# A four-block model on one Trainium2 core: where the attention's weighted values and adapter scores are transposed, and into which banks

## Chip, cores and metric

The kernel runs on one core of a Trainium2 chip. The core has TensorE (PE, matrix products and transposes, with its own queue of weight loads, PEld), VectorE (DVE), ScalarE (ACT), GpSimd (POOL) and the queues that start transfers (SP among them). The metric is the device time of one execution in microseconds (us); lower is better. Products and transposes land in PSUM, which has eight banks of 2 KB for each of the 128 partitions: a bank takes 512 float32 numbers a partition.

## The reference, cut to what matters

The input is 4 sequences of 256 tokens with 512 channels. Four blocks follow each other; the change is in the first, an attention with 32 heads of 16 channels and an adapter: ten learned extra keys and values with a softmax of their own, gated and added.

```
q, k, v = split(layernorm(x) @ w_attn.T); q, k = rope(q), rope(k)
scores  = q @ k.T / sqrt(hd)                    # causal mask, hd = 16
y       = softmax(scores) @ v
ascores = gating * softmax(q @ ak.T / sqrt(C))  # ak, av: 10 adapter keys and values per head
y       = (y + ascores @ av) @ w_proj.T
x = x + y
x = x + ffn(layernorm(x)); x = x + mixer(layernorm(x)); x = x + ffn(layernorm(x))
```

## The kernel before, in words

All of the attention lies in one function. The 4 sequences (batches, b) are done in 8 steps of 4 heads each (u), 32 steps i = 8b + u in one loop. Four heads share the 128 partitions in PE's array, 32 rows a head. For one step there are these stages; line numbers are those of the kernel before.

1. *Scores* (L492): 16 products into four PSUM banks (pool of 4, tile `sc`), one bank a head, of which 384 of 512 columns are used: 256 columns for the second half of the queries (c = 1), 128 for the first (c = 0). DVE reads them in eight reduces (L500), which add the causal mask, write the scores to on-chip memory as `e` and leave the row maximum in `nmx`. ACT then takes eight exponentials (L508).
2. *turn* (L523), one step later: 12 transposes of the exponentials into three banks `ptr`, copied out as `eT` (L524), the first and third by ACT and the second by DVE.
3. *weigh* (L533, L539), two steps later: the exponentials times the values into the bank `py`; a column of ones among the values gives the softmax's sum. DVE copies py out as `ys` (L547, function `taken`).
4. *gathered* (L553), three steps later: two transposes `try` turn ys back to tokens on partitions; DVE takes the reciprocal of the sum, `ry` (L558), and multiplies into the batch's result `y` (L559). `y` has one buffer: the next batch's first write must wait until the batch before is read out.

Beside that runs, in steps of even u (except the very first step) and once at the start, the adapter: *adapter_scores* makes products `pa` (L457), ACT copies them out as `sa` (L462), two transposes `tra` (L466) turn them, and ACT copies the result into the batch's `as` (L467). There are four such pieces a batch. After the fourth, at u = 7, *adapted* (L570 to L577) makes the adapter's softmax on all of `as`: a maximum `anm` on DVE, an addition on POOL, an exponential on ACT, sum `asum`, reciprocal and scaling on DVE, a multiplication on POOL. In the next batch's first step its transposes `pt` (L584) follow, and then its products with the adapter values, `pya`.

*closed* adds the two parts of a batch and turns the result for the output projection (transposes `try2`, named try in the profile, L610, with copies `yT`, L107 and L108). Three quarters of it are done in the step in which the batch's seventh `gathered` is finished (steps 10, 18, 26), the last one a step later (steps 11, 19, 27); its transposes go into the stage "turn", at a step's end.

Other long products (`pq` for queries, keys and values of the next batch, `po`, and parts of the next block) are placed by hand into the stage "long" of a step (12 products of 128x512, L115 to L117); transposes of the queries and keys (`trp`, L444, copied out as `pc` and swapped by DMA) come just after the scores.

The order on PE is written out by hand in the loop. In a step i it is: scores(i), adapter products, trp, long products, weigh(i - 2), turn(i - 1), try of gathered(i - 3), tra, then the stage "turn" (pt, the transposes of the next normalised rows `tr`, the closed batch's try2). The order on DVE, ACT and POOL is made by a scheduler from the dependencies.

Of the eight PSUM banks three are a rotating pool "m": ptr, try, tra, try2, pa, pt, pq, trp and the rest take its banks in turn, and a transpose into a bank waits until the copy out of it three tiles earlier is done. Four are the score banks, one tile each, and one is for py.

Of the kernel before, what the change touches and what calls it, by code (L numbers as in the profile page):

```python
# [20 lines left out]
P = 128  # L21
# [58 lines left out]
def hybrid_kernel(  # L80
# [190 lines left out]

    def attention(later, region):
        with ExitStack() as es:
            inner, banks = ExitStack(), ExitStack()
            pool = lambda name, bufs, **kw: es.enter_context(tc.tile_pool(name=name, bufs=bufs, **kw))
            w1 = pool("a_w", 1)
            p1 = pool("a1", 1)
            p2 = pool("a2", 2)
            p3 = pool("a3", 3)
            ps, ps_s, ps_y = (  # L280
                banks.enter_context(tc.tile_pool(name=name, bufs=bufs, space=PSUM))
                for name, bufs in (("a_m", 3), ("a_s", 4), ("a_y", 1))
            )

            acon = w1.tile([P, NCOL_ATTN - NCOL_KEEP], F32, name="acon")
# [150 lines left out]
            def pieces(b, q, f):  # L436
# [13 lines left out]
                turned_.setdefault((b, q), []).append(o)  # L450
                yield

            def adapter_scores(b, q):
                pa = ps.tile([AW, L], F32, name="pa", tag="m")
                for j in range(4):
                    n = (4 * q + j) * AW
                    nc.tensor.matmul(  # L457
                        pa, akbd[:, n : n + AW], turned_[b, q][0][:, 0, j % 2, :],
                        start=(j == 0), stop=(j == 3),
                    )  # L460
                sa = p2.tile([AW, 4, P], F32, name="sa", tag="paT").rearrange("p s i -> p (s i)")[:, :L]
                nc.scalar.copy(sa, pa)  # L462
                yield
                tr = ps.tile([P, 2, AW], F32, name="tra", tag="m")
                for c in range(2):
                    nc.tensor.transpose(tr[:, c, :], sa[:, c * P : (c + 1) * P], ident[:AW, :AW])  # L466
                nc.scalar.copy(  # L467
                    state[b]["as"][:, :, q * 8 : q * 8 + 8, :].rearrange("p c h a -> p c (h a)"), tr
                )
# [11 lines left out]
            def scores(b, u):  # L481

                qT, kT = turned_[b, u // 2]
                es_ = [p2.tile([P, 4, (c + 1) * P], F32, name=f"e{c}", tag=f"e{c}") for c in range(2)]
                tops = {}
                banks_ = [ps_s.tile([P, 3, P], F32, name="sc", tag="sc") for _ in range(4)]
                for c, at in ((1, slice(0, 2)), (0, slice(2, 3))):
                    n = (c + 1) * P
                    for v in range(2):
                        for r in range(4):  # L490
                            rows = slice(32 * r, 32 * r + 32)
                            nc.tensor.matmul(  # L492
                                banks_[r][:, at, :].rearrange("p k i -> p (k i)"),
                                qT[rows, 0, u % 2, c * P : (c + 1) * P], kT[rows, v, u % 2, :n],
                                start=(v == 0), stop=(v == 1),
                            )
                for c, at in ((1, slice(0, 2)), (0, slice(2, 3))):
                    tops[c] = nm = p3.tile([P, 4], F32, name="nmx", tag="nmx", bufs=4)
                    for r in range(4):
                        nc.vector.tensor_tensor_reduce(  # L500
                            es_[c][:, r, :].rearrange("p (k i) -> p k i", i=P), banks_[r][:, at, :],
                            mask[:, 1 - c :, :], -1.0, 3e38, ALU.add, ALU.min, nm[:, r : r + 1],
                        )

                yield
                for c in (1, 0):
                    for r in range(4):
                        nc.scalar.activation(  # L508
                            es_[c][:, r, :], es_[c][:, r, :], AF.Exp, scale=-1.0, bias=tops[c][:, r : r + 1],
                        )  # L510
                    if c == 0:
                        all_es[8 * b + u] = es_
                    yield
# [34 lines left out]
                return ys  # L548

            def gathered(b, u, ys):  # L550
                tr = ps.tile([P, 2, 4, 32], F32, name="try", tag="m")
                for c in range(2):
                    nc.tensor.transpose(  # L553
                        tr[:, c].rearrange("p h d -> p (h d)"), ys[:, c * P : (c + 1) * P], ident
                    )
                st = state[b]
                ry = p2.tile([P, 2, 4], F32, name="ry")
                nc.vector.reciprocal(ry, tr[:, :, :, HD])  # L558
                nc.vector.tensor_tensor(  # L559
                    st["y"][:, :, 64 * u : 64 * u + 64].rearrange("p c (h d) -> p c h d", h=4),  # L560
                    tr[:, :, :, :HD], ry.unsqueeze(3).to_broadcast([P, 2, 4, HD]), ALU.mult,
                )
# [137 lines left out]
                norm.stats(t, tc.keep_in_program_order)  # L700
            norm.root(2, TT)
            begin(0)
            for f in range(2):
                for _ in pieces(0, 0, f):
                    pass
            part = pieces(0, 1, 0)
            next(part)
            moved(adapter(), -1)
            with tc.manual_schedule(engines={nc.tensor.engine}):
                for i in range(n):  # L710
                    b, u = divmod(i, 8)
                    if u == 0:
                        if i:
                            begin(b)
                        if b + 1 < B:
                            moved(prepared(b + 1), i)
                    scoring = scores(b, u)
                    next(scoring)
                    if i in FEEDS:
                        moved(fed(feed, FEEDS[i]), i - 1)  # L720
                    if i == 2:
                        nc.scalar.activation(a_s, a_s, AF.Exp)
                        nc.gpsimd.tensor_scalar(a_s, a_s, -1.0, None, ALU.mult)
                    if i == 3:
                        weights(wp_s, wproj, "ya", nc.gpsimd, p1)
                    if u % 2 == 0 and i > 0:
                        asides.append(adapter_scores(b, u // 2))
                        next(asides[-1])
                    if part:
                        next(part)  # L730
                    part = None
                    next(scoring)
                    step("long", i)
                    step("values", i)
                    if 2 <= i:
                        py = weigh(*divmod(i - 2, 8), eTs.pop(i - 2))
                    if 1 <= i:
                        eTs[i - 1] = turn(all_es.pop(i - 1))
                    next(scoring)
                    if 2 <= i:  # L740
                        yss[i - 2] = taken(py)
                    if 3 <= i:
                        gathered(*divmod(i - 3, 8), yss.pop(i - 3))
                    while asides:
                        next(asides.pop(0), 0)
                    step("turn", i)
                    if u == 7:
                        moved(adapted(b), i)
                    if 3 <= i:
                        if (i - 3) % 8 == 6:  # L750
                            moved(closed((i - 3) // 8, (0, 1, 2)), i)
                        if (i - 3) % 8 == 7:
                            moved(closed((i - 3) // 8, (3,)), i)

                    b, u = divmod(i + 3, 8)
                    if b < B:
                        part = pieces(b, u // 2, (i + 1) % 2)
                        next(part)
                    if i == 23:
                        inner.close()  # L760
                        feed = Feed("f", *(
                            later.enter_context(
                                tc.tile_pool(name=f"f{v}", bufs=v, side="right", reuse_waits="tile")
                            ) for v in (1, 2)
                        ))
                    if i in range(23, 27):
                        feed.weights(i - 23, nc.gpsimd)
                        feed.norm.stats(i - 23)
                    if i == 26:
                        feed.norm.root(0, 4)  # L770
# [3 lines left out]
                step("long", n)  # L774
                yss[n - 2] = taken(weigh(b, 6, eTs.pop(n - 2)))
                eTs[n - 1] = turn(all_es.pop(n - 1))
                gathered(b, 5, yss.pop(n - 3))
                step("turn", n)
                moved(fed(feed, 3), n - 1)
                step("turn", n)  # L780
                step("long", n + 1)
                step("values", n + 1)
                yss[n - 1] = taken(weigh(b, 7, eTs.pop(n - 1)))
                gathered(b, 6, yss.pop(n - 2))
                moved(closed(b, (0, 1, 2)), n)
                moved(fed(feed, 4), n)
                step("turn", n + 1)
                gathered(b, 7, yss.pop(n - 1))
                moved(closed(b, (3,)), n)
                step("long", n + 2)  # L790
                step("turn", n + 2)
# [1120 lines left out]
```

## Time and profile before

| what | us |
|---|---|
| median of 3 runs | 1805.35 (1804.81 to 1807.16) |
| profiled execution | 1805.61 |
| its span | 1803.8 |
| first scores of the loop to the last step's scores | 31.7 to 280.6 |
| PE busy from 28 to 318 | 262.88 of 290.00 |

The steps have different lengths, since the long products differ. The start of the score products, read from PE's timeline:

| step | 10 | 11 | 12 | 13 | 18 | 19 | 20 | 26 | 27 | 28 |
|---|---|---|---|---|---|---|---|---|---|---|
| first score product at | 117.67 | 126.03 | 132.99 | 140.36 | 181.11 | 189.41 | 196.38 | 243.91 | 250.38 | 255.07 |

ScalarE's row for the copy of the adapter scores is one of the operations that move in order: all 16 of them in the trace.

```profile
L467 ACT COPY as<-tra x16: 281/292/298, 64.7 to 279.9; 128x160 f32<-128x160 f32 x16
L570 DVE TENSOR_REDUCE anm<-as x4: 819/820/821, 93.6 to 280.3; 128x64 f32<-128x640 f32 x4
L571 POOL TENSOR_TENSOR as<-as,anm x4: 1293/1300/1529, 94.5 to 281.2; 128x640 f32<-128x640 f32 x4
L584 PE MATMUL pt<-con,as x32: 272/273/280, 106.5 to 299.5; 128*80 128x128 f32 x32
```

In this view, of all that touches the tile `as`, the three numbers after the count are the shortest, the median and the longest duration in ns, followed by the start of the first and the last of them in us and the operands' shapes. In a timeline the columns are start, duration, engine, line, operation, written tile and read tiles, count; in square brackets stands how long the engine was idle before, and what it waited for.

### The profile page before, as it was taken

To read this page: it belongs to the slowest core of one execution; us is meant where nothing else is said; L and a number is where in the kernel's file an instruction comes from. 1 tells how busy PE (TensorE), PEld (TensorE's weight loads), DVE (VectorE), ACT (ScalarE), POOL (GpSimd) and SP (SyncE) were. 2 spreads that over 40 slices of the span, in tenths; PEclk is the share of its full clock that TensorE was granted. 3 is DMA by queue.
4 is the path that set the end of the run, shared out by engine and by line. 5 is a ranking of instruction groups with operands and counts; after the bars stand their busy time and mean duration, and the time that the engine had idled before them with its cause. 6 is when DMAs were issued, how large, how long until landed. Compare 5 with 4: busy or idle time off the path is not lost.

```text
span 1803.8 us, 33220 instructions
## 1 busy us (share of the span) xinstructions
PE 1745.7 (97%) x12862; PEld 1417.8 (79%) x12862; DVE 1427.7 (79%) x2523; ACT 1268.7 (70%) x2293; POOL 240.9 (13%) x249
## 2 busy tenths in 40 slices
PE   7999988899999999999999999999999999999998
PEld 6777767778877888888888888888888888888877
DVE  5676676889998788787878797878788878887777
ACT  5676684578887668766866686668667867777754
POOL 5332320111110111011110101110111101101100
PEclk8999999999999999999999999999999999999999
DMA  4000100122344234423433252325333433343231
GB/s 157 19 19 19 47 26 26 43 71 99 109 127 137 80 106 154 120 85 99 153 100 100 88 162 90 109 81 176 103 94 112 135 106 94 115 138 115 85 97 56
DMA packets 136941, 173.71 MB, mean 96 GB/s; under 512 B 12752, under 2 KB 78032, under 8 KB 136784
## 3 DMA queue, kind: packets, MB, share of 16 engines
q1 hardware_dynamic: 127712, 138.57, 25.5%
q10 hardware_dynamic: 9072, 33.03, 4.8%
q8 instruction: 101, 1.65, 0.4%
q14 instruction: 56, 0.46, 0.1%
HBM read 131.71 MB, written 35.65 MB: 93 GB/s over the span
## 4 chain that ended last, share of the span: by engine, by line
PE 76%; DVE 11%; ACT 8%; issue 3%; DMA 1%; POOL 1%; SPq 0%; ACTq 0%; DVEq 0%; POOLq 0%
PE pp L115 13%; PE pp L117 12%; PE pp L116 12%; PE pyy L1252 7%; PE pog L115 6%; PE pog L117 6%; PE pog L116 6%; PE trx L1233 3%; DVE acc L980 2%; ACT e L508 1%; ACT em L1213 1%; DVE em L1226 1%; PE pq L115 1%; PE ptr L523 1%; PE pq L117 1%
## 5 line engine op out<-in xcount | busy, mean ns | idle before, releaser
L115 PE MATMUL pp<-mx,w 128*128 128x512 f32 x1144 | 459.3, 401 | 0.0
L117 PE MATMUL pp<-mx,w 128*128 128x512 f32 x1144 | 446.8, 391 | 0.0
L116 PE MATMUL pp<-mx,w 128*128 128x512 f32 x1144 | 446.1, 390 | 0.0
L1285 POOL TENSOR_TENSOR sq<-sq,x 128x1024 f32<-128x1024 f32 x54 | 132.1, 2446 | 1177.7 <-ACT x L1284 1177.7
L117 PEld LDWEIGHTS pp<-mx,w 128*128 128x128 f32 x1144 | 214.7, 188 | 46.2
L115 PEld LDWEIGHTS pp<-mx,w 128*128 128x128 f32 x1144 | 214.8, 188 | 44.7
L980 DVE SCALAR_TENSOR_TENSOR acc<-pp,cw_s,acc 128x1012 f32<-128x1012 f32 (+2 forms) x192 | 244.5, 1274 | 4.3
L116 PEld LDWEIGHTS pp<-mx,w 128*128 128x128 f32 x1144 | 215.1, 188 | 40.5
L1226 DVE TENSOR_TENSOR em<-em,gm 128x1280 f32<-128x1280 f32 x128 | 189.5, 1489 | 72.1 <-ACT em L1221 72.1
L115 PE MATMUL pog<-wo,gh 128*128 128x512 f32 x512 | 201.2, 393 | 2.0 <-DVE x L1381 2.0
L117 PE MATMUL pog<-wo,gh 128*128 128x512 f32 x512 | 200.2, 391 | 0.9 <-DVE gh L1364 0.9
L116 PE MATMUL pog<-wo,gh 128*128 128x512 f32 x512 | 199.8, 390 | 0.0
L1236 DVE TENSOR_TENSOR xd<-trx,dt_t 128x512 f32<-128x512 f32 x128 | 82.4, 685 | 141.5 <-PE trx L1233 141.5
L1152 ACT ACT_TABLE_LOAD x63 | 80.8, 1283 | 139.1 <-DVE acc L980 138.9
L1443 ACT ACTIVATE gt<-pp 128x1024 f32<-128x1024 f32 x64 | 65.6, 1025 | 145.0 <-PE pp L117 145.0
L1252 PEld LDWEIGHTS pyy<-em,xd 64*64 64x64 f32 x4096 | 130.2, 133 | 44.2 <-issue 17.6
L1213 ACT ACTIVATE em<-r,end_t 128x128 f32<-128x128 f32 x512 | 163.1, 389 | 0.8
L1252 PE MATMUL pyy<-em,xd 64*64 64x256 f32 (+3 forms) x4096 | 157.8, 300 | 3.1 <-DVE em L1226 3.0
L115 PEld LDWEIGHTS pog<-wo,gh 128*128 128x128 f32 x512 | 96.3, 188 | 24.8 <-issue 2.8
L508 ACT ACTIVATE e<-e,nmx 128x256 f32<-128x256 f32 (+1 forms) x256 | 97.2, 448 | 24.3 <-DVE nmx L500 24.2
L117 PEld LDWEIGHTS pog<-wo,gh 128*128 128x128 f32 x512 | 96.4, 188 | 22.3 <-DVE gh L1364 2.1
L116 PEld LDWEIGHTS pog<-wo,gh 128*128 128x128 f32 x512 | 96.4, 188 | 19.5
(324 smaller groups left out, 3094.5 us busy)
## 6 DMA issues: line engine op xcount, KB each, us to landing
wr<-in_win_dram SPq DMA_DIRECT2D x144, 256.0 KB, 2.7
r<-cumd SPq DMA_DIRECT2D x256, 128.0 KB, 2.9
spill<-gb ACTq DMA_DIRECT2D x63, 512.0 KB, 2.8
gr<-spill SPq DMA_DIRECT2D x120, 256.0 KB, 3.4
wor<-in_wout_dram SPq DMA_DIRECT2D x64, 256.0 KB, 4.4
pc<-pc SPq DMA_DIRECT2D x32, 128.0 KB, 2.0
out_dram<-x SPq DMA_DIRECT2D x7, 256.0 KB, 2.3
x<-in_x_dram SPq DMA_DIRECT2D x1, 1536.0 KB, 9.0
```

Of the source, the lines that this page charges most:

```text
L115: nc.tensor.matmul(o, lh, rh, start=(first and k == 0), stop=False)
L116: nc.tensor.matmul(o, lh, rl, start=False, stop=False)
L117: nc.tensor.matmul(o, ll, rh, start=False, stop=(last and k == n - 1))
L508: nc.scalar.activation(es_[c][:, r, :], es_[c][:, r, :], AF.Exp, scale=-1.0, bias=tops[c][:, r : r + 1],)
L980: nc.vector.scalar_tensor_tensor(av[:, :, d:], pv[:, :, : L - d], cw_s[:, ch, tap : tap + 1], av[:, :, d:], ALU.mult, ALU.add,)
L1152: nc.scalar.activation(pair(x2).rearrange("p k u i -> p u k i"), acc.rearrange("p (u k i) -> p u k i", u=2, i=Q), AF.Silu,)
L1213: nc.scalar.activation(piece(e, j, c, 2 - c, 2), rv[:, j, 2:, :], AF.Exp, bias=end_t[:, 2 * j + c, h : h + 1],)
L1226: nc.vector.tensor_tensor(e, e, gm, ALU.mult)
L1236: nc.vector.tensor_tensor(xd[:, hs, :].rearrange("p c (h d) -> p c h d", h=2), tr.rearrange("p c (h d) -> p c h d", h=2), dt_t[:, hs, 2 * ...
L1252: nc.tensor.matmul(py[d, u, j * L + c * Q : (j + 1) * L].rearrange("p (k i) -> p k i", i=Q), xd[us, 4 * j + c, d], piece(es2[hh], j, c)[us ...
L1285: (nc.gpsimd if n < NB - 2 else nc.vector).tensor_tensor(sqs[g], sqs[g], x2, ALU.add)
L1443: nc.scalar.activation(gts[i], pp, AF.Silu)
```

## The change

The four score banks become one tile, `four`, of 128 partitions x 4 banks x 4 quarters x 128 columns. The scores use quarters 0 to 2 of each bank as before. The transposes `try` go into quarter 3 of banks 0 and 1, the transposes `tra` (80 columns each) into quarter 3 of banks 2 and 3; neither takes a bank of the rotating pool any more. The long products of the first batch, which shared the score pool before the loop, keep it until the loop begins; then that pool is closed and the one-tile pool opened in its place.

On PE both kinds of transposes move from the end of step i - 1 or i to the head of step i, ahead of its score products: `try` of gathered(i - 3), whose ys was copied out in step i - 1, and the `tra` of the adapter piece begun in step i - 1. What reads them (ry, y and the copy as) comes in the program after the score products and ahead of the reduces. In step 3 two adapter pieces are pending: the first is turned at the head, the second after the scores. After the loop, `gathered` of the last three steps is done as before.

```diff
-            ps, ps_s, ps_y = (
-                banks.enter_context(tc.tile_pool(name=name, bufs=bufs, space=PSUM))
-                for name, bufs in (("a_m", 3), ("a_s", 4), ("a_y", 1))
+            ps, ps_y, ps_s = (
+                (opening if name == "a_s" else banks).enter_context(
+                    tc.tile_pool(name=name, bufs=bufs, space=PSUM)
+                )
+                for name, bufs in (("a_m", 3), ("a_y", 1), ("a_s", 4))
             )
...
             def adapter_scores(b, q):
...
                 yield
-                tr = ps.tile([P, 2, AW], F32, name="tra", tag="m")
+                tr = four[:, 2:4, 3, :AW]
                 for c in range(2):
                     nc.tensor.transpose(tr[:, c, :], sa[:, c * P : (c + 1) * P], ident[:AW, :AW])
+                yield
                 nc.scalar.copy(
                     state[b]["as"][:, :, q * 8 : q * 8 + 8, :].rearrange("p c h a -> p c (h a)"), tr
                 )
...
             def scores(b, u):
...
-                banks_ = [ps_s.tile([P, 3, P], F32, name="sc", tag="sc") for _ in range(4)]
...
                             nc.tensor.matmul(
-                                banks_[r][:, at, :].rearrange("p k i -> p (k i)"),
+                                four[:, r, at, :].rearrange("p k i -> p (k i)"),
                                 qT[rows, 0, u % 2, c * P : (c + 1) * P], kT[rows, v, u % 2, :n],
                                 start=(v == 0), stop=(v == 1),
                             )
+                yield
...
                         nc.vector.tensor_tensor_reduce(
-                            es_[c][:, r, :].rearrange("p (k i) -> p k i", i=P), banks_[r][:, at, :],
+                            es_[c][:, r, :].rearrange("p (k i) -> p k i", i=P), four[:, r, at, :],
...
             def gathered(b, u, ys):
-                tr = ps.tile([P, 2, 4, 32], F32, name="try", tag="m")
+                tr = four[:, 0:2, 3, :].rearrange("p c (h d) -> p c h d", d=32)
                 for c in range(2):
                     nc.tensor.transpose(
                         tr[:, c].rearrange("p h d -> p (h d)"), ys[:, c * P : (c + 1) * P], ident
                     )
+                yield
...
             begin(0)
+            opening.close()
+            four = banks.enter_context(
+                tc.tile_pool(name="a_f", bufs=1, space=PSUM, reuse_waits="tile")
+            ).tile([P, 4, 4, P], F32, name="sc")
...
+                    aside = [gathered(*divmod(i - 3, 8), yss.pop(i - 3))] if 3 <= i else []
+                    for j in aside + asides[:1]:
+                        next(j)
                     scoring = scores(b, u)
+                    next(scoring)
+                    for j in aside + asides[:1]:
+                        next(j, 0)
+                    for j in asides[1:]:
+                        next(j)
+                        next(j, 0)
+                    asides.clear()
                     next(scoring)
...
                     if 2 <= i:
                         yss[i - 2] = taken(py)
-                    if 3 <= i:
-                        gathered(*divmod(i - 3, 8), yss.pop(i - 3))
-                    while asides:
-                        next(asides.pop(0), 0)
                     step("turn", i)
...
-                gathered(b, 5, yss.pop(n - 3))
+                whole(gathered(b, 5, yss.pop(n - 3)))
```

A helper `whole` runs such a generator to its end; it is used where `gathered` and `pieces` are not split.

## The prediction

> **What bounds the kernel now.** I read the busy shares first, then the chain of work that ended last, then what TensorE (PE) waits for in the attention part, then the timelines of single steps there. Times are from the start of the span; line numbers are those of the kernel before.
>
> ```profile
> span 1803.8 us, 33220 instructions
> PE 1745.7 (97%) x12862; PEld 1417.8 (79%) x12862; DVE 1427.7 (79%) x2523; ACT 1268.7 (70%) x2293; POOL 240.9 (13%) x249
> PE 76%; DVE 11%; ACT 8%; issue 3%; DMA 1%; POOL 1%; SPq 0%; ACTq 0%; DVEq 0%; POOLq 0%
> ```
>
> PE is busy 97% of the span, so microseconds are won or lost where PE stands still. The change touches only the attention loop: 32 steps, from 31.7 to 281 us, and the tail to about 318. PE is busy for 262.88 of the 290 us from 28 to 318. What follows is PE-bound and shifts as a whole. The waits of PE in that window, the longest groups:
>
> ```profile
> engine line waited for: us in total, times, longest us
> PE try L553 <- ACT eT L524: 5.0, 7, 2.2
> PE ptr L523 <- DVE fx L248: 2.7, 3, 1.6
> ...
> PE ptr L523 <- ACT av L431: 1.3, 1, 1.3
> ```
>
> The first group is what moving `try` can win: the transposes at a step's end take the next of three rotating banks and wait for ScalarE (ACT) to empty it. With the 0.4 us of try behind VectorE (DVE) and 0.5 us of tra that makes 5.9 us. The end of an ordinary step and of a new batch's fourth step (step 11), on PE:
>
> ```profile
> 130.75 1.53 PE L523 MATMUL ptr<-con,e 128*128 128x128 f32 x12
> 132.14 0.44 PE L553 MATMUL try<-con,ys 128*128 128x128 f32 x2
> 132.63 0.44 PE L610 MATMUL try<-con,y 128*128 128x128 f32 x2
> 132.99 0.68 PE L492 MATMUL sc<-pc,pc 32*128 32x256 f32 x16
> ```
>
> PE has nothing ahead of it but its own order. DVE at the same place:
>
> ```profile
> 132.61 0.21 DVE L558 RECIPROCAL ry<-try 128x8 f32<-128x8 f32 x1
> 133.10 0.29 DVE L559 TENSOR_TENSOR y<-try,ry 128x128 f32<-128x128 f32 x1 [0.28 <-PE try L610]
> 133.50 0.42 DVE L108 TENSOR_TENSOR yT<-try,yT 128x256 fp32r<-128x256 f32 x1
> 133.85 0.41 DVE L500 CUSTOM_DVE_ANT_0 e<-sc,acon 128x256 f32<-128x256 f32 x1
> ...
> 136.06 0.08 DVE L500 DVE_READ_ACCUMULATOR2_ANT nmx<- 128x1 f32 x1
> ```
>
> The product y (L559) of a new batch's first step writes a `y` with one buffer, and waits until PE has turned the old batch's last piece (L610). It costs 0.28 us now, because both stand at the step's end.
>
> **The change, part by part.** No operation is added or dropped; PE's two try and two tra transposes move from a step's end to its head. All four score banks become one tile, with try and tra in its fourth quarter. In the changed kernel's built order every reader of this tile waits for other users of it, whichever bank they touch: ry waits for the step's last score product, y for ry, the adapter copy `as` (L467, ACT) for y, the eight reduces (L500) for that copy or y, and the next head's transposes for the reduces.
>
> *Ordinary steps.* Before, the reduces began 0.71 to 1.0 us after the first score product. Now ry (0.21) and y (0.29) come first, from 0.68: the reduces begin at about 1.3, and in odd steps, where pc (0.57) and as (0.29) come between on ACT, at about 2.05. Their exponentials are needed only when the next step turns them, 2 to 7 us later, which hides this. Gained are the try and tra waits: 5.9 us in all, of which 2.2 lies in step 23 (counted below) and the rest partly returns as waits for the same copies at the next transposes that need the bank. Bounds -3.7 and 0; I take -1.5.
>
> *Steps 11, 19, 27, the largest term.* y of the new batch (now read from the head's try) still needs the L610 transposes, which stay at the end of the same step. as waits for y, all eight reduces for as, and PE's next head waits for the last reduce. From step 11's first score product at 126.03, by the rows above: L610 starts at 6.60 (now at 6.1, since try no longer stands before it), y 0.47 later, 6.57 to 6.87; ACT's cast of yT (0.37) ends at 6.95, as (0.29) at 7.25 to 7.6; the reduces take 2.29 (133.85 to 136.14), to 9.6 to 10.1; the head's try goes 0.36 to 0.4 ahead of the scores, which start at 10.0 to 10.5. They started at 6.96. Loss 3.1 to 3.6, taken 3.4. Step 19 has the same rows. Step 27 is short, 4.69 us to the next scores: L610 is ready at about 4.1, yT 4.5, as 4.8, the reduces 7.25, scores 7.6; loss 2.9, less the 0.7 that the next scores then lost to a transfer (0.46 of it shows as a DMA wait), 2.2. Together 9.0, bounds 8.2 to 10.1. Behind the waiting DVE stand all its later rows; ACT's exponentials of that step run while PE already works on the next.
>
> *Half clock after those stalls.* Each leaves PE idle for 2.5 to 3.3 us. The trace has such gaps:
>
> ```profile
> 230.10 0.52 PE L553 MATMUL try<-con,ys 128*128 128x128 f32 x2 [2.22 <-ACT eT L524]
> 230.55 1.12 PE L492 MATMUL sc<-pc,pc 32*128 32x256 f32 x16
> 231.60 1.14 PE L457 MATMUL pa<-pc,akbd 128*80 128x256 f32 x4
> ```
>
> In the windows of that place the granted clock is 0.53 from 230.10 for 3.41 us, against 1.00 before the gap; score products take 1.12 instead of 0.68 and pa 1.14 instead of 0.70. The excess over the usual times sums to about 1.6 us. A gap of 1.33 at 100.3 was not followed by it. The idles to come are longer than 2.22, so I take 3 x 1.6 = 4.8; bounds 0 (the gate misses them) and 3 x 3.4 (each as after 288.36, where 6.83 us ran at 0.50).
>
> [...]
>
> *The adapter chain, steps 7 to 10, 15 to 18, 23 to 27.* as of the eighth step comes late (2.05 after the scores), so the chain behind it does: DVE's anm (0.82) now follows the step's reduces, to 5.25; POOL's add (1.30) to 6.6; ACT's exponential (0.74) behind an eT copy, to 8.3; asum, reciprocal and scaling (0.82 + 0.55 + 0.25) to 10.0. They stand in DVE's order ahead of step 8's ry, y and reduces, which end at 12.8; step 8's first exponentials stand on ACT ahead of the eT copy that frees the bank for `pt` (L584), at 13.5. PE would get there at 10.0: idle 3.5, plus half clock. Gone in exchange: the 1.3 behind av, the try waits of 0.3 and 0.9, the pt and tr waits of 0.2 to 0.6, and in step 23 the 2.2 with its 1.6 of half clock. Net by block +1.1, +1.6 and -1.0: +1.7; bounds -4 (all these waits gone, pt not late) and +6 (nothing absorbed).
>
> *Single places.* Step 3 has two adapter pieces; the second can be turned only when the first is copied, after the scores: 0.68 + 0.3 + 0.29 + the hand-overs, +1.4 (0 to 1.6). In step 5 an eT copy (0.69) goes ahead of ys on DVE, and the next head's try waits for ys: +0.8 (0 to 0.8). In the tail, where ptr waited 1.6 for DVE and half clock followed, step 31's reduces come sooner: -1.0 (-3.5 to 0).
>
> **Sum.** 9.0 + 4.8 + 1.7 + 1.4 + 0.8 - 1.5 - 1.0 = +15.2. The profiled execution took 1805.61 (span 1803.8 and 1.8 around it), 0.26 above the median of the runs: 1805.35 + 15.2 = 1820.5 us.
>
> [...] In the trace before, reduces at 102.22 to 104.1 and copies out of other banks (ACT sa at 103.15) ran at once. [...]
>
> **Rivals.** (1) *The waits go and none comes*: try and tra no longer wait for a rotating bank, and the late reduces are hidden even in steps 11, 19 and 27. For it: 5.9 us of such waits, two of the long ones on steps before the chain. Against: the built order's wait of y for L610 and of the next head for the last reduce. It decides if y is ready by the time the scores end. Price -5.9, so 1799.5: the faster side. (2) *The three stalls without half clock*, the chain neutral: 1805.35 + 9.0, with the single places and gains cancelling: 1814. For it: the gap of 1.33 without a clock loss; against: that of 2.22 with it. (3) *The chain's pt stalls in full*, two or three times 3.5 + 1.6 less what goes: +6 instead of +1.7, and half clock lasting longer at one stall: 1820.5 + 4.3 + 1.8 = 1826.6. For it: DVE's order as built; against: PE's waits of about 3 us in each block that disappear. (4) *Nothing to see*: y of the first step of a batch, late in its step, is absorbed by later waits: 1805. Against: between step 12 and step 15 PE waits nowhere that could absorb 3 us.
>
> **How the numbers follow.** Forecast 0.59, rival 2 0.18, rival 3 0.13, rival 1 0.05, rival 4 0.05. The range reaches from between rivals 4 and 2 to above rival 3: 1810 to 1829; its low end takes the three stalls at 8.2 with the gains at their better ends (-3.5), its high end rival 3 with the three stalls at 10.1 and the gains of ordinary steps at -0.3. About 0.2% (3.6 us) is what can be told from no change. Faster by more than that: 0.05 (rival 1), within it 0.05 (rival 4), slower 0.90.
>
> **What would show it.** Right: in steps 11, 19 and 27 PE idle of 2.4 to 3.6 us before try, released by a reduce or the as copy, and clock 0.50 behind it; y waiting several us for L610; in step 8 and 16 pt waiting for eT about 3 us; no more waits of try for eT at a step's end. Wrong: step 12's scores 7 us behind step 11's, no clock loss behind idles over 2.5 us, or the reduces of ordinary steps so late that turning waits for exponentials in most steps, which would put the time over 1830.

## The result, and the profile after

| | us |
|---|---|
| before, median of 4 runs | 1805.08 (1804.24 to 1807.16) |
| changed kernel, median of 4 runs | 1818.12 (1816.97 to 1818.87) |
| ratio, 95% interval | 1.0070 (1.0053 to 1.0087) |
| profiled execution, its span | 1818.44, 1816.6 |

The changed kernel is 13 us slower. The head of its profile page, and its chain of work by engine:

```profile
span 1816.6 us, 33196 instructions
PE 1747.3 (96%) x12862; PEld 1423.9 (78%) x12862; DVE 1427.3 (79%) x2523; ACT 1270.1 (70%) x2293; POOL 240.7 (13%) x249
PE 79%; DVE 10%; ACT 6%; issue 2%; DMA 1%; POOL 1%; SPq 0%; ACTq 0%; DVEq 0%; POOLq 0%
```

Every engine has the same number of instructions and nearly the same busy time; the span grew by 12.8 us, so PE stands still for longer. What it waits for between 28 and 332 us, the longest groups of the changed kernel (total us, times, longest):

```profile
PE sc L561 <- ACT e L516: 10.5, 3, 3.5
PE sc L499 <- DMA pc<-pc: 3.9, 3, 2.3
PE pt L593 <- POOL st L345: 3.8, 2, 2.6
PE pt L593 <- ACT eT L532: 2.6, 2, 2.2
...
PE sc L473 <- ACT as L475: 1.3, 1, 1.3
```

L561 is the head's try, now written into the tile named sc; L593 is pt, L475 the as copy. The group of try at a step's end that led the list before is gone, and a group of three waits of 3.5 us stands in its place. The releasers that the view names, an exponential and POOL's st, are only the last events ahead of the wait; the timelines show the real ones. The first of the three, at the end of step 11, on PE, then DVE, then ACT (start, duration, engine):

```profile
135.21 0.44 PE L619 MATMUL try<-con,y 128*128 128x128 f32 x2
139.12 0.42 PE L561 MATMUL sc<-con,ys 128*128 128x128 f32 x2 [3.48 <-ACT e L516]
139.48 1.12 PE L499 MATMUL sc<-pc,pc 32*128 32x256 f32 x16
```

```profile
133.15 0.69 DVE L325 TENSOR_TENSOR t<-pq,acon 128x512 f32<-128x512 f32 x1 [3.10 <-PE pq L117]
...
135.69 0.29 DVE L568 TENSOR_TENSOR y<-sc,ry 128x128 f32<-128x128 f32 x1
136.34 0.42 DVE L108 TENSOR_TENSOR yT<-try,yT 128x256 fp32r<-128x256 f32 x1 [0.36 <-ACT yT L107]
136.68 0.41 DVE L508 CUSTOM_DVE_ANT_0 e<-sc,acon 128x256 f32<-128x256 f32 x1
...
138.69 0.28 DVE L508 CUSTOM_DVE_ANT_0 e<-sc,acon 128x128 f32<-128x128 f32 x1
```

```profile
136.19 0.31 ACT L475 COPY as<-sc 128x160 f32<-128x160 f32 x1
```

The chain reads off the start times: PE turns the old batch's last piece (135.21), y follows (135.69), then as (136.19), the reduces (136.68 to 138.97), and 0.15 us later PE goes on. The scores had been ready since 129.8, and DVE had sat idle for 3.10 us before 133.15 with the reduces held back. The score products after the stall take 1.12 us. The clock around it, in three stretches of 3.41 us (PE busy, PEld, DVE, ACT, POOL, then the granted clock, where 1.00 is full and 0.50 is called half clock here, DMA share, GB/s):

```profile
132.56:135.97 3.41, 3.09 (x33) 2.02 (x31) 2.66 (x6) 1.11 (x3) 1.27 (x1) 1.00 0.10 38
135.97:139.38 3.41, 0.26 (x2) 0.20 (x2) 2.65 (x18) 2.78 (x10) 0.00 (x0) 1.00 0.00 0
139.38:142.79 3.41, 3.41 (x28) 3.10 (x27) 2.10 (x13) 1.61 (x6) 0.82 (x3) 0.50 0.00 0
```

PE is busy for 0.26 of 3.41 us, and the next 3.41 us run at 0.50.

Where the 12.8 us of the span come from, worked out from the start of each step's scores in the two traces (after less before, change from step to step):

| place | predicted | measured |
|---|---|---|
| before step 3 | 0 | +0.45 |
| step 3 to 4, second adapter piece | +1.4 | +1.45 |
| step 5 to 6, ys behind an eT copy | +0.8 | +0.82 |
| steps 11, 19, 27, to the next scores | 3.4 + 3.4 + 2.2 = 9.0 | 3.41 + 3.65 + 3.69 = 10.75 |
| the step after each, half clock | 4.8 | 1.06 + 2.32 + 1.50 = 4.88 |
| adapter chain, steps 7 to 11, 15 to 19, 23 to 27 | +1.1 + 1.6 - 1.0 = +1.7 | +1.1 + 1.3 + 0.5 = +2.9 |
| all other steps | -1.5 | -2.8 |
| from step 31's scores to the end | -1.0 | -5.6 |
| sum | +15.2 | +12.8 |

The adapter chain shows in step 8 of the changed kernel as a wait of pt on PE, behind a sum of the adapter's softmax on DVE that stands ahead of the step's reduces (these begin at 104.77, 3.26 us after the first score product at 101.52; before it was 0.71):

```profile
107.55 1.04 PE L593 MATMUL pt<-con,as 128*80 128x128 f32 x8 [2.17 <-ACT eT L532]
```

```profile
102.72 0.82 DVE L583 TENSOR_REDUCE asum<-as 128x64 f32<-128x640 f32 x1 [1.05 <-ACT as L581]
```

Half clock (0.50) follows from 108.67 for 6.83 us.

### The profile page after: what moved, and what is told of

Same layout as the page of the kernel before. It is cut to its first block, busy times and chain, and to the rows that moved or that the text cites. A ratio compares the mean times of both kernels' runs of the same rounds, so it can differ in the third digit from the quotient of the medians.

```text
span 1816.6 us, 33196 instructions
## 1 busy us (share of the span) xinstructions
PE 1747.3 (96%) x12862; PEld 1423.9 (78%) x12862; DVE 1427.3 (79%) x2523; ACT 1270.1 (70%) x2293; POOL 240.7 (13%) x249
## 3 DMA queue, kind: packets, MB, share of 16 engines
q8 instruction: 101, 1.65, 0.4%
## 4 chain that ended last, share of the span: by engine, by line
PE 79%; DVE 10%; ACT 6%; issue 2%; DMA 1%; POOL 1%; SPq 0%; ACTq 0%; DVEq 0%; POOLq 0%
PE pp L115 13%; PE pp L117 13%; PE pp L116 13%; PE pyy L1270 7%; PE pog L115 6%; PE pog L116 6%; PE pog L117 6%; PE trx L1251 3%; PE ptr L531 1%; DVE acc L998 1%; PE pq L115 1%; ACT e L516 1%; PE pq L116 1%; PE pq L117 1%; DVE em L1244 1%
## 5 line engine op out<-in xcount | busy, mean ns | idle before, releaser
L938 DVE TENSOR_TENSOR w<-wr,w 128x512 fp32r<-128x512 f32 x138 | 99.4, 725 | 4.4 <-ACT w L935 4.4
```

Of the source, the lines that this page charges most:

```text
L938: nc.vector.tensor_tensor(w[1], r, w[0].bitcast(F32), ALU.subtract)
```

## The experiments

All but one alter the changed kernel, most of them in one part; times are medians, ratios are against the kernel before run on the same chip. Where a step is said to start late, it is against the kernel before, counted from the step ahead of it, in the profiled execution.

**Two buffers for y.** The wait of y is taken away by giving the new batch another buffer.

```diff
-                    "y": p1.tile([P, 2, C], F32, name="y"),
+                    "y": p1.tile([P, 2, C], F32, name="y", bufs=2),
```

> The changed kernel with two buffers for y, so that a new batch's first product into y need not wait until the old batch's last piece is turned; nothing else differs. Theory (the three large stalls come from that wait, passed on through the as copy and the reduces): in steps 11, 19 and 27 the next scores follow after 7.0, 7.0 and 4.7 us instead of 10.4, 10.6 and 8.4; the stalls (10.8 us by the step starts) and the half clock after them (4.9) go, so 1818.1 - 15.7 = about 1802.5, and the clock stays at 1.00 at those places. Rival (the loss comes from readers kept apart in every step, the y wait is only where it shows): the three steps shorten by less than 1 us each, 1815 or more.

Measured: 1802.22, ratio 0.9984 (0.9971 to 0.9998). Steps 12 and 20 start 0.35 and 0.32 us later against the kernel before than the step ahead of them, instead of 3.41 and 3.65, and behind step 11 the score products take 0.69 us, not the 1.12 of half clock. Step 11 to 12 on PE in this kernel:

```profile
136.03 0.38 PE L619 MATMUL try<-con,y 128*128 128x128 f32 x2
136.35 0.44 PE L561 MATMUL sc<-con,ys 128*128 128x128 f32 x2
136.72 0.69 PE L499 MATMUL sc<-pc,pc 32*128 32x256 f32 x16
```

The head follows the last piece at once. One buffer for y, which cost 0.28 us on DVE before, cost the changed kernel some 16 us. Step 28 still starts 1.59 late: PE waits 1.29 us there for an eT copy ahead of the last piece, and, other than expected, a stretch of 3.41 us at half clock follows (0.50 from 262.65), behind one of 3.42 us in which PE was busy for 2.35.

**The kernel before with two buffers for y**, the same edit there, as a control.

> The kernel before with two buffers for y, nothing else. Theory (there the wait for the old batch costs the 0.28 us that the trace shows, on DVE, three times, and PE does not wait for it): 1805.1 - 0.5 at most, within noise of before, about 1804.8. Rival (two buffers gain by themselves what the run with two y buffers showed over before): about 1802.

Measured: 1805.42, ratio 1.0007 (0.9995 to 1.0020). The buffer gains nothing by itself.

**The move alone.** Both transposes go to the head, but into rotating banks, and the scores keep a tile for each bank.

```diff
-                tr = four[:, 2:4, 3, :AW]
+                tr = ps.tile([P, 2, AW], F32, name="tra", tag="m")
...
-                tr = four[:, 0:2, 3, :].rearrange("p c (h d) -> p c h d", d=32)
+                tr = ps.tile([P, 2, 4, 32], F32, name="try", tag="m")
...
+                banks_ = [ps_s.tile([P, 3, P], F32, name="sc", tag="sc") for _ in range(4)]
...
-                                four[:, r, at, :].rearrange("p k i -> p (k i)"),
+                                banks_[r][:, at, :].rearrange("p k i -> p (k i)"),
```

> Only the move: try and tra go to the head of the step as in the changed kernel, but into the rotating banks as before, and the scores keep four tiles of a bank each. Theory (the loss comes from the sharing of one tile, not from the place): y still waits in steps 11, 19, 27, but no reduce waits for it; the waits of try for the rotating banks stay as in the kernel before: 1805, between 1801 and 1808. Rival (the later place itself costs, since y and as come a head later): 1812 or more, with the stalls in steps 11, 19 and 27 still there.

Measured: 1807.01, ratio 1.0013 (1.0003 to 1.0024). Step 12 starts 0.92 late, step 20 0.89, not 3.4 and 3.7. In sum the loop is 6.7 us longer by its step starts and what follows it 5.5 shorter, so the place, with rotating banks, costs about a tenth of a per cent; the sharing of one tile makes the rest of the 0.70%.

**tra back at the step's end**, in a rotating bank; try stays shared.

```diff
-                tr = four[:, 2:4, 3, :AW]
+                tr = ps.tile([P, 2, AW], F32, name="tra", tag="m")
...
-                    for j in aside + asides[:1]:
+                    for j in aside:
...
                         yss[i - 2] = taken(py)
+                    while asides:
+                        whole(asides.pop(0))
                     step("turn", i)
```

> The changed kernel with the adapter transposes tra put back to the step's end and into the rotating banks; try stays at the head in the shared banks. Theory (the adapter chain and step 3 are late because the as copy waits for y and for the scores; the three stalls are passed on by y standing ahead of the reduces on DVE too): the three stalls stay, shorter by the as copy and the yT cast, about 0.7 each; step 8's and 16's waits of pt (2.2 and 2.5 us with half clock in blocks 7 to 10, 15 to 18, 23 to 27, net +2.5) and step 3's +1.45 go, the tra waits come back (+0.5): 1818.1 - 2.1 - 2.5 - 1.4 + 0.5 = about 1812.5. Rival (the three stalls hang on the as copy alone): about 1800. Rival (the chain is late by the reduces, not by the as copy): 1816.

Measured: 1812.42, ratio 1.0048 (1.0033 to 1.0063), the number expected, but by terms that cancel: the three stalls and the steps behind them gained 5.5 us by the step starts and not 2.1, the adapter chain gained less than expected, and the tail lost 3.6. The three stalls are there without as, shorter by 0.8 to 1.7:

```profile
132.02 0.44 PE L619 MATMUL try<-con,y 128*128 128x128 f32 x2
135.06 0.44 PE L561 MATMUL sc<-con,ys 128*128 128x128 f32 x2 [2.60 <-DVE nmx L508]
```

So the wait also passes from y straight to the reduces, by DVE's order. Step 3's loss is gone (-0.05 instead of +1.45). The chain's blocks went to -0.5, +1.5 and +0.6, in sum 1.4 us better and not 2.5, since waits of ptr for av (1.9) and for x (2.1) stand where the waits of pt were. From step 31's scores to the end this kernel took 1521.2 us; the kernel before took 1523.25, the changed kernel 1517.6. That bears on the tail's gain: with tra at the step's end DVE does the last batch's asum (0.82) ahead of step 31's reduces, here as in the kernel before, and PE waits 1.6 us for DVE behind them; with tra at the head the reduces go first.

**Half clock, first try.** Idle products (ones into the spare py bank, not used) on PE inside the three stalls.

```diff
                     step("turn", i)
+                    if i in (11, 19, 27):
+                        warmed(ps_y.tile([P, L], F32, name="wy", tag="py"), [ident] * 26)
```

> The changed kernel with 26 idle products (ones into the spare py bank) on PE at the end of steps 11, 19 and 27, some 2.9 us each, inside the stall and over before the reduces end; what they write is not used. Theory (PE's idle time of 3.4 us brings the half clock): the half-clock stretches at 139.4, 207.7 and 272.5 are gone, the stalls themselves stay; steps 12, 20 and 28 lose 1.1, 2.3 and 1.5 us less: 1818.1 - 4.9 = about 1813. Rival (the half clock has another cause, or the idle products delay the next head): the stretches stay and the time is 1818 or more.

Measured: 1814.21, ratio 1.0056 (1.0041 to 1.0071). Near the expected time, but two effects partly cancel in it: each product ran as two matmuls, 52 of them for 5.97 us, and held up the next head by 2.1 us (step 12 +5.54 instead of +3.41), while the steps behind gained. It does not size the half clock, so it was run again with fewer.

**Half clock, 12 products.**

> As the run with idle products, but 12 instead of 26 at each place: each of them runs as two matmuls of 0.115 us, so 26 took 5.97 us and held up the next head by 2.1; 12 take 2.75 and end before the last reduce. Theory (the half clock comes from PE's idle time in the stall): steps 12, 20 and 28 start as late as in the changed kernel (+3.4, +3.7, +3.7), the clock stays at 1.00 behind them, and the steps after lose nothing: 1818.1 - 6.8 = about 1811. Rival (the gain in the run before came from somewhere else): 1814 or more.

Measured: 1806.36, ratio 1.0006 (0.9992 to 1.0019). The first of the three places, on PE:

```profile
131.65 0.44 PE L619 MATMUL try<-con,y 128*128 128x128 f32 x2
131.92 2.84 PE L122 MATMUL wy<-con,ones 128*128 128x128 f32 x24
135.56 0.41 PE L561 MATMUL sc<-con,ys 128*128 128x128 f32 x2 [0.80 <-ACT e L516]
135.90 0.68 PE L499 MATMUL sc<-pc,pc 32*128 32x256 f32 x16
```

The stalls stay (+3.41, +3.40, +3.44). At the first the granted clock is 1.00 from 131.90 to 139.40 and the score products behind it take 0.68 and not 1.12. The next steps change by -0.36, -0.35 and -1.23 where they had lost 1.06, 2.32 and 1.50: by these differences half clock cost 1.42 + 2.67 + 2.73 = 6.8 us. The time expected was 1811; the median fell by 11.8 us, 5 more than the 6.8. Of the 10.9 us between the two profiled executions 7.7 lie in the loop, and 3.2 come from the first scores, which started at 28.97 instead of 32.17, ahead of all that was edited. That start lies between 28.97 and 32.73 in the profiles of this study, and differences of 3 us between single kernels are not read as effects here.

**Two tiles of two banks.** try shares with heads 0 and 1, tra with heads 2 and 3.

```diff
-            ).tile([P, 4, 4, P], F32, name="sc")
+            )
+            four = [four.tile([P, 2, 4, P], F32, name=f"sc{j}") for j in range(2)]
...
-                tr = four[:, 2:4, 3, :AW]
+                tr = four[1][:, :, 3, :AW]
...
-                                four[:, r, at, :].rearrange("p k i -> p (k i)"),
+                                four[r // 2][:, r % 2, at, :].rearrange("p k i -> p (k i)"),
```

> The changed kernel with the one tile cut in two of two banks each: try shares with the scores of heads 0 and 1, tra with those of heads 2 and 3; y keeps one buffer. Theory (the readers are kept apart by tile, whichever bank they touch, so half as large tiles take the as copy and half of the reduces out of the wait for y): in steps 11, 19 and 27 only the last reduces follow y, the next head starts 1.5 to 2.1 us earlier than in the changed kernel, PE idles 1.5 to 2 us, less than half of a clock window, and the half clock behind it goes: 1818.1 - 6.0 - 4.9 = about 1807, up to 1810. Rival (as and y meet on the banks themselves, or the stall is y's wait alone): the three steps lose 3.4 us and more as before, 1816 or more.

Measured: 1794.79, ratio 0.9945 (0.9928 to 0.9963): 0.55% faster than the kernel before, and 12 us better than expected. Step 11 in it, DVE and PE:

```profile
131.56 0.29 DVE L568 TENSOR_TENSOR y<-sc,ry 128x128 f32<-128x128 f32 x1
131.77 0.41 DVE L508 CUSTOM_DVE_ANT_0 e<-sc,acon 128x256 f32<-128x256 f32 x1
...
133.09 0.29 DVE L508 CUSTOM_DVE_ANT_0 e<-sc,acon 128x128 f32<-128x128 f32 x1
```

```profile
133.02 0.44 PE L561 MATMUL sc<-con,ys 128*128 128x128 f32 x2 [1.49 <-DVE nmx L508]
```

Two of the eight reduces are over before y, the others follow y at once, since as is not between them, and the head waits only for the reduces of its own tile. The next scores are 1.44, 1.44 and 1.42 us late, and the score products behind the first of these waits take 0.73 us, not 1.12. What the expectation left out is the adapter chain: as is copied ahead of pc, pt waits 1.11 us in steps 8 and 16 instead of 2.17 and 2.58, and steps 9, 17 and 25 change by -0.04, -0.04 and +1.65 where they lost 1.18, 2.64 and 4.50. The mean granted clock of the execution is 0.990, in the changed kernel 0.985. In sum the chain's three blocks go from +2.9 to -6.2. Step 6 no longer loses its 0.82.

**Three smaller steps.** Step 3's second piece turned at the head of step 4:

```diff
-                    for j in asides[1:]:
-                        next(j)
-                        next(j, 0)
-                    asides.clear()
+                    del asides[:1]
```

> Two buffers for y, and the second adapter piece of step 3 is turned at the head of step 4 instead of behind step 3's scores. Theory: step 4 no longer starts 1.45 us late, nothing else moves: 1802.2 - 1.4 = about 1800.8. Rival (the wait for the first as copy moves to step 4's head): 1802.2.

Measured: 1802.76, ratio 0.9977 (0.9966 to 0.9987), not told apart from the run without it. In the trace the wait of 1.3 us for as is gone, but waits of 0.24 for an eT copy and 0.22 for ys came in its place; step 4 starts 1.01 instead of 1.45 late. Neither theory was quite right.

With two buffers for y and only try in the shared banks, tra at the head in a rotating one:

```diff
-                tr = four[:, 2:4, 3, :AW]
+                tr = ps.tile([P, 2, AW], F32, name="tra", tag="m")
...
-                    for j in aside + asides[:1]:
+                    for j in aside + asides:
                         next(j)
```

> Two buffers for y, both transposes at the head, but only try in the score banks; tra takes a rotating bank. The as copy then waits neither for y nor for the scores, and the reduces not for it. Theory: against the run with two y buffers step 4's 1.45 goes and the adapter chain comes earlier (blocks 7 to 10, 15 to 18, 23 to 27 about 1.5 better in sum, as in the run with tra at the end), tra's waits for a rotating bank cost 0.5: 1802.2 - 2.5 = about 1800; if the tail falls back to the old order (the chain's sum ahead of step 31's reduces on DVE) up to 3.6 more, 1803.5. Rival (the as copy's place does not matter): 1802 with step 8 and 16 waiting 2.2 and 2.5 us for pt as before.

Measured: 1800.55, ratio 0.9978 (0.9966 to 0.9990), as expected, though within the spread of the run with two y buffers. PE's waits for av (1.9 us) and x (2.2 us) are back here.

**The best of it**: two tiles, two buffers for y, and step 3's piece deferred, the three edits shown above together.

> Two tiles of two banks, two buffers for y, and step 3's second adapter piece turned at step 4's head. Theory: the waits of y that are left in steps 11, 19 and 27 (1.44, 1.44 and 1.42 us at the next scores) fall to what the run with two y buffers had there (0.35, 0.32 and 1.59), and step 4's 0.58 goes: 1794.8 - 2.7 = about 1792. Rival (nothing left in those waits that PE feels): 1794.8.

Measured: 1788.32, ratio 0.9907 (0.9891 to 0.9922), the fastest of the study, 0.9% under the kernel before and 4 us under what was expected. Steps 12 and 20 now start 0.27 and 0.28 us earlier against the kernel before than the step ahead of them; step 28 is still 1.09 late.

And with the last piece turned a step earlier in place of the second buffer:

> As the run before, but with one buffer for y: the last piece of a batch is turned one step earlier (steps 10, 18 and 26, with the other three pieces), so that the next batch's first y finds its buffer free. Theory (what counts is that the old batch is read out before y, not the second buffer): the same 1792, within 2 us; the fourth piece in step 10 waits for a rotating bank, 0.3 to 0.8 us each time. Rival (the y wait needs the second buffer): 1795 or more.

```diff
+                    if 3 <= i and (i - 3) % 8 == 7:
+                        moved(closed((i - 3) // 8, (3,)), i - 1)
                     step("turn", i)
...
-                        if (i - 3) % 8 == 7:
-                            moved(closed((i - 3) // 8, (3,)), i)
```

Measured: 1791.44, ratio 0.9925 (0.9913 to 0.9938). What counts is that the old batch is read out before y, with or without a second buffer; the price is the fourth transposes of steps 10, 18 and 26 (+0.51, +0.57 and +1.58 at the next scores, the last one twice what was expected).

## Why the prediction was right, and where its sizes were off

The forecast, 1820.5, was 2.4 us above the median, and its mechanism is what the runs show; that the sum came so close is in part luck, since errors of several us in its terms cancel. Point by point:

- *The three stalls.* Right, and the largest term. The wait of y for the old batch is the cause: with a second buffer it goes, with the control showing that the buffer alone does nothing. The way it is passed on, by as and by DVE's order, is shown by the run with tra at the end. Step 11 went as laid out: from its first score product (129.11) y came at 6.58, the end of as at 7.39, the reduces' end at 9.86 and the next scores at 10.37. Step 27 was mis-sized, 3.69 instead of 2.2. From the step's first score product (264.73) I put the end of the yT cast at 4.5, of as at 4.8, the reduces' end at 7.25 and the next scores at 7.6; they came at 4.98, 5.17, 7.64 and 8.39, the last also because the head's try, from 272.52, already ran at half clock (0.50 from 272.50; 0.60 us to the scores instead of 0.36). And the 0.7 us of a transfer wait that I took off belongs to the next step: in the kernel before it lies behind step 28's first products (255.91), not ahead of them.
- *Half clock.* Right in kind, too small in size: 4.8 taken, 6.8 measured by the idle products. The sum of step starts hides it (4.88), because the same steps gain 0.35, 0.35 and 1.2 in the run with 12 idle products. Rival 2, the stalls without half clock at 1814, falls.
- *The adapter chain.* Right: DVE did asum ahead of step 8's reduces, pt waited 2.17 us (3.5 predicted) and 6.83 us at half clock (0.50) followed. In sum +2.9 for +1.7. That as, late, starts it is supported by the run with two tiles, where as goes first and the blocks come to -6.2; moving tra back gained only 1.4 us, since other waits returned.
- *Single places.* Steps 3 and 5: right to 0.05 us. The control of step 3 shows the cause but not the gain.
- *Ordinary steps*: -2.8 for -1.5. In the kernel before, the reduces began 1.33 to 1.38 us after the first score product in seven steps (9, 10, 17 and 18 among them) and later still in steps 28, 30 and 31, not at most 1.0, as I had read it. In the changed kernel they began at 1.2 to 1.6 in most even steps and at 2.0 in most odd ones, near what was predicted, and in the ordinary steps this was hidden, as argued.
- *The tail* was mis-sized most: -5.6 for -1.0, beyond its bounds of -3.5 and 0. In the kernel before, step 31's reduces began at 284.26, 3.7 us after its scores; in the changed kernel 2.1 us after. ptr waits 0.35 instead of 1.60 and 0.27 (rows below), and the 6.83 us at 0.50 from 288.36, worth some 3.4 us (an estimate, half of them), are gone; the changed kernel has 3.41 us at 0.50 from 347.60. The kernel before with two y buffers, with the same order and the same wait of 1.6, needed 1520.6 from step 31's scores, 2.6 less than the kernel before. Its mean granted clock over the whole execution was 0.992 against 0.989, so I put those 2.6 of the 5.6 us down to the clock and the rest to the order, a rough estimate: where in that execution the clock was lower is not shown. I had counted the wait, and too little of the clock. This error and the two that were too small (stall and chain, 3 us) partly cancel: the total is better than its terms.
- Rival 1, the faster side, is what appears when the y wait and the shared tile are cut back: 1794.8 to 1788.3. Its 5.9 us were the right thing to look for, but the gain in the tail and around the chain is larger. Rival 3 fell short, rival 4 falls.

The waits of ptr in the tail, in the kernel before and in the changed kernel:

```profile
287.59 0.66 PE L523 MATMUL ptr<-con,e 128*128 128x128 f32 x4 [1.60 <-DVE fx L248]
288.51 0.87 PE L523 MATMUL ptr<-con,e 128*128 128x128 f32 x3 [0.27 <-DVE fx L248]
```

```profile
305.20 0.66 PE L531 MATMUL ptr<-con,e 128*128 128x128 f32 x4 [0.35 <-ACT eT L532]
```

Sharing one tile does cost (ratio 1.0070, against 1.0013 for the move alone), but most of the cost here is not one of banks: with the same two banks for each transpose, in two tiles, the kernel is faster than before (0.9945). What held readers of different banks apart was the tile as the unit of the waits. What is left within a tile, 1.4 us at each of the three places, may be the tile or the bank: no run gave each bank a tile, and none opened the pool without `reuse_waits="tile"`, so neither is settled.

The chain's cost by itself is not shown. In the two forms that share try but give tra a rotating bank, asum is out of the way (with tra at the step's end it starts at 97.07, step 8's reduces at 103.20), and pt waits at most 0.6 us in steps 8 and 16. Yet their blocks are only 1.4 and 1.0 us better than those of the same kernels with tra in the shared tile, and other waits, for av and x, stand there instead.

## What to carry to other kernels

Parking another result in an unused corner of a buffer joined its readers here to all readers of that buffer: list each wait that any of them has, in every phase, and look for the rare one (here a single-buffered output at a batch's turn, 0.28 us before, 3.5 us after). Cut the shared tile along the lines in which it is used before giving the idea up: two tiles instead of one turned +0.70% into -0.55%. And count a stall of PE with the half clock that may follow it: here that was 6.8 us on 10.3 us of stalls.

## What the runs showed of the hardware

Times in this section are from the traces of the kernel before and of the changed kernel where no other run is named. Between 60 and 345 us the stretches at half clock (0.50) last 3.41 or 6.83 us. In the kernel before they begin at 230.33, 288.36 and 332.73, so 58.03 and 44.37 us apart, which is 17 and 13 times 3.413; in the changed kernel at 108.67, 139.38, 176.93, 207.65, 245.20 and 272.50, which is 9, 11, 9, 11 and 8 times 3.413 us apart. The 3.41 us just ahead of half clock were not always idle. From the kernel before:

```profile
226.92:230.33 3.41, 0.88 (x6) 0.62 (x6) 1.93 (x5) 3.41 (x9) 1.25 (x1) 1.00 0.21 79
230.33:233.74 3.41, 3.41 (x34) 2.72 (x36) 2.57 (x18) 3.35 (x5) 3.41 (x6) 0.50 0.00 0
```

PE's busy share of those 3.41 us, in the order of the starts above, was 0.26, 0.50 and 0.55 in the kernel before and 0.36, 0.08, 0.27, 0.02, 0.37 and 0.00 in the changed kernel. Counted on from the same starts in steps of 3.413 us, the lowest shares with no half clock behind them are 0.53, from 248.61 in the changed kernel, and 0.61, from 97.21 in the kernel before. With two buffers for y a stretch of 0.69, from 259.23, had half clock behind it. So in these runs the share alone does not decide.

Nor does the length of a gap. With two buffers for y half clock followed PE's wait of 1.29 us ahead of step 28. In the kernel before it followed the waits of 1.60 us ahead of 287.59 and of 2.22 us ahead of 230.10, but the clock stayed at 1.00 behind the wait of 1.33 us ahead of 100.31. The wait of 1.49 us in the run with two tiles had score products of 0.73 us behind it, not of 1.12.
